# All left sides of a two-layer graph-attention kernel are turned through DRAM and VectorE's square transposes, and the hand-written order is made anew

## The chip, the cores and the metric

The kernel runs on one core of a Trainium2 chip. Such a core has a matrix engine (TensorE, "PE" in the profile, its weight loads "PEld"), a vector engine (VectorE, "DVE"), a scalar engine (ScalarE, "ACT"), a general engine (GpSimd, "POOL") and a sequencer that here issues the transfers (SyncE, "SP"). Each engine runs its own list of instructions strictly in the order in which they were written, and they meet only through semaphores. Transfers between DRAM and on-chip memory run on 16 DMA engines. The metric is the device time of one execution in microseconds (us); the number compared is the median of the runs.

## The reference

Two graph layers run over 64 graphs of 256 nodes with 512 features. Each layer normalizes its input, clips it at zero, and adds the result of an attention network over the graph's adjacency matrix:

```python
h = jnp.maximum(_layernorm(x, axis=-1), 0.0)
x = x + _L0_gnn_ref(adj, h, W1, att_src1, att_dst1, b1, W2, att_src2, att_dst2, b2)
h = jnp.maximum(_layernorm(x, axis=-1), 0.0)
x = x + _L1_gnn_ref(h, adj, W_proj, W_att, b_att)

def gat_layer(x, mask, W, a_src, a_dst, bias, concat):      # inside _L0_gnn_ref, called twice
    xl = (x @ W).reshape(B, N, H, F)
    e = leaky_relu(asrc[:, :, None, :] + adst[:, None, :, :], 0.2)
    attn = softmax(where(mask[..., None], e, -1e9), axis=1)
    out = einsum('bsdh,bshf->bdhf', attn, xl)
```

The first network has two such layers: 512 features to 4 heads of 256 (W1) with an ELU after it, then 1024 features to one head of 512 (W2). The second has one layer of 8 heads of 64 (W_proj), with the mask's rows and columns exchanged and a clip at zero at its end. Everything is float32.

## The kernel before

The graphs are independent and are worked on as a pipeline. The class `Graph` (L292) has one method for each small step, and three strings (`head`, `order`, `tail`, L638 to L690) name the steps in the order in which their instructions are recorded; `run` (L693) reads them. In an item such as `-1 gat3 0 1` the first number says which graph, counted from the round's number, and the rest is the method and its arguments. `order` runs once for each round from 2 to 62, so a steady round holds the steps of several graphs at different stages, one graph's worth in all. An item that begins with `w` prepares weights. This written order alone sets the place of every instruction on every engine; no scheduler moves anything (L125).

A graph's stages are, with their steps:

- `load` fetches x (tile `xs`, two buffers) and the adjacency `ad`; `stats1` and `norm1` make the normalized `h` on DVE, POOL and ACT; `masks` makes two 0/1 masks in bfloat16 from `ad` on DVE (L308, L310); `caps` turns one of them into limits on ACT, and `cap3` transposes it by DMA.
- `m1a`, `m1b` multiply h by the two halves of W1, `m2` the ELU's result z by W2, `m3` the second h by W_proj. Each is a `Product` (L38): a 2x2 blocked product with seven block products instead of eight, whose steps are p1, p2, p5, p6, p7, p4, p3 on PE, and c22. Four sums of blocks of the left side come first, from `left` on POOL (L212); the block products read the left side's seven blocks `a[:, i]`: p1 block 0, p2 block 1, p6, p5, p7 blocks 2, 3, 4 (the sums), p4 block 5, p3 block 6. ACT keeps partial sums (`kept`, L60) and DVE adds them (`total`, L260). The PSUM tiles are `sum` (two buffers) and `pm` (four).
- The attention's weights: `exp1`, `exp2`, `exp3` on ACT, then `rows1`, `rows2`, `rows3`, which call `spread` (L233): a small DVE transpose (L237), a write of 16 KB to DRAM, and reads that broadcast rows to all partitions (`bc`). `edges1`, `edges2`, `edges3` make the weight matrices `e` (ACT L289, then DVE L290), `gat1`, `gat2`, `gat3` multiply by them on PE, `out1`, `out2`, `out3` scale the results. `elu1` finishes the ELU of one half of z's columns for one half of the nodes: `elu1 g t` with g the columns' half and t the nodes' half. `store` writes the result.

A left side must lie with the features on the partitions, so it has to be turned. Before the change there are two ways. h of layer 1 (`away`, `back`) and the first half of z (`send2`, `back2`) take a trip: they are written to DRAM in blocks and read back rearranged, and DVE then transposes squares of 32x32 (`nc.vector.transpose`, L209, L430). The second half of z (`turn2`) and the h of layer 3 (`turn3`) are turned on PE with an identity (L196), and ACT copies them out of PSUM (L229, L441). The first and the last graph take PE for more. The read that ends a trip directly follows its write in SP's list, and so waits there until the write has landed:

```python
        kept = dram.tile([T, 4, P, P], F32, name="kept_h")
        nc.sync.dma_start(kept.rearrange("t a p e -> p t a e"), h.rearrange("p t (a e) -> p t a e", a=4))
        nc.sync.dma_start(h, kept.rearrange("t a (j q) e -> (a j) t (q e)", q=4))
```

`bias` adds b2 to `xs`, and `out2` adds the first network's result to it, into `x2` (two buffers), which `store` writes in the end.

## Time and profile before

| what | value |
|---|---|
| median of 3 runs | 3147.14 us (3146.95 to 3150.41) |
| span of the profiled execution | 3144.0 us; its own time is not listed apart from the runs |
| PE / DVE / ACT / POOL busy in the span | 97% / 78% / 60% / 40% |
| DMA engines, mean busy share in the middle | 39%, 112 GB/s |
| one round (one graph), from one step to the same step a graph later | 47.5 us |
| PE transposes in all | 1044 |

The span runs from the first to the last instruction. A busy share is an average over the span; what an engine is worth at some place is read from what waits there. In the groups by form a row shows line, engine, operation, tiles and shapes, the count, then after a bar the busy time in all and the mean duration in ns of one instruction, and after a second bar the idle time of the engine before these instructions with what ended it. Means of instructions that overlap with the next one are longer than what one of them costs; the distance between the starts of two steps in the timeline is the cost. In the timeline a row gives start, duration from the first start to the last end, engine, line and operation. SP's waits count from the end of its instruction before.

### The profile page before, as it was taken

How to read it: one execution, taken by the hardware profiler on the slowest of the kernel's cores; microseconds unless marked ns; L12 is line 12 of the kernel's file. 1: busy time of each engine (PE TensorE's matmuls, PEld its weight loads, DVE VectorE, ACT ScalarE, POOL GpSimd, SP SyncE). 2: the span in 40 equal slices, each digit the busy share in tenths (PEclk: the TensorE clock that was granted, in tenths of full speed). 3: DMA queues.
4: the chain of work that ended last, by engine and by line, in shares of the span. 5: the costliest groups of instructions: out<-in, count | busy, mean ns of one | idle time of the engine just before them, and what ended most of it. 6: DMA issues, size and time to landing. Idle time of an engine off the chain costs nothing. (4 is left out here: it accounts for less than half of the span.)

```text
span 3144.0 us, 60657 instructions
## 1 busy us (share of the span) xinstructions
PE 3064.8 (97%) x21312; PEld 2628.9 (84%) x21312; DVE 2466.5 (78%) x6503; ACT 1882.1 (60%) x4743; POOL 1245.5 (40%) x1434
## 2 busy tenths in 40 slices
PE   4899999999999999999999999999999999999997
PEld 3788888888888888888888888888888888888886
DVE  7588788787787787787787887887887877877875
ACT  2466666665666666566566666566666656666664
POOL 1443433433433434434434434434434334334342
PEclk8999999999999999999999999999999999999999
DMA  4234443333433433434433333433444334334331
GB/s 138 71 110 113 117 107 115 118 108 105 126 102 111 127 102 111 127 100 113 120 106 112 116 106 114 115 109 117 108 116 117 107 109 123 105 108 127 102 112 36
DMA packets 350779, 346.49 MB, mean 110 GB/s; under 512 B 78600, under 2 KB 236168, under 8 KB 350472
## 3 DMA queue, kind: packets, MB, share of 16 engines
q1 hardware_dynamic: 349096, 340.45, 37.6%
q8 instruction: 174, 2.85, 0.4%
q10 hardware_dynamic: 1376, 2.10, 0.2%
q14 instruction: 133, 1.09, 0.1%
HBM read 231.87 MB, written 102.20 MB: 106 GB/s over the span
## 5 line engine op out<-in xcount | busy, mean ns | idle before, releaser
L289 ACT ACTIVATE wy<-bc,exs_sb 128x256 f32<-128x256 f32 x1646 | 731.7, 500 | 261.7 <-DVE e L290 148.3
L260 DVE TENSOR_TENSOR xl<-pm,kept 128x256 f32<-128x256 f32 (+2 forms) x768 | 318.1, 421 | 414.6 <-PE pm L54 395.5
L60 ACT ACTIVATE kept<-sum 128x264 f32<-128x264 f32 (+3 forms) x768 | 294.4, 383 | 419.1 <-PE sum L54 416.2
L394 PE MATMUL pm<-xl,e 128*128 128x257 f32 x2048 | 498.6, 387 | 20.6 <-DVE e L290 15.1
L528 POOL TENSOR_TENSOR x<-x,o 128x256 f32<-128x256 f32 x256 | 196.4, 768 | 788.8 <-DVE o L526 770.2
L54 PE MATMUL sum<-w_sb,h1s 128*128 128x257 f32 x2048 | 489.7, 381 | 7.7 <-POOL h1s L216 7.1
L290 DVE SCALAR_TENSOR_TENSOR e<-wy,exs_sb,cap 128x256 f32<-128x256 f32 x1024 | 446.9, 479 | 56.0 <-ACT wy L289 56.0
L394 PEld LDWEIGHTS pm<-xl,e 128*128 128x128 f32 x2048 | 369.3, 190 | 100.2 <-PE pm L394 28.3
L54 PEld LDWEIGHTS sum<-w_sb,h1s 128*128 128x128 f32 x2048 | 380.6, 191 | 67.1 <-POOL h1s L216 7.5
L54 PE MATMUL pm<-w_sb,h1s 128*128 128x257 f32 x1536 | 365.4, 380 | 1.2 <-DVE xl L260 1.0
L181 POOL TENSOR_TENSOR rstd<-ve,neg_half 128x2 f32<-128x2 f32 x128 | 116.8, 912 | 622.0 <-DVE ve L179 622.0
L54 PEld LDWEIGHTS pm<-w_sb,h1s 128*128 128x128 f32 x1536 | 291.1, 190 | 45.4 <-issue 1.4
L290 DVE SCALAR_TENSOR_TENSOR e<-wy,exs_sb,mask 128x256 f32<-128x256 f32 x640 | 302.4, 523 | 5.2 <-ACT wy L289 5.2
L518 PEld LDWEIGHTS pm<-xl,e 128*64 128x64 f32 x8192 | 250.6, 138 | 47.3 <-issue 22.7
L54 PE MATMUL sum<-w1b_sb,hs 128*128 128x256 f32 x1024 | 266.7, 384 | 7.8 <-DVE w1b_sb L554 5.0
L54 PE MATMUL sum<-w1a_sb,hs 128*128 128x260 f32 x1024 | 268.7, 385 | 5.7 <-DVE w1a_sb L554 3.3
L54 PE MATMUL sum<-wp_sb,hs 128*128 128x264 f32 x1024 | 270.6, 387 | 3.0 <-ACT kept L60 2.5
L518 PE MATMUL pm<-xl,e 128*64 128x65 f32 x8192 | 269.2, 224 | 3.9 <-DVE e L290 2.9
L404 DVE SCALAR_TENSOR_TENSOR z<-pm,r,b_sb 128x256 f32<-128x256 f32 x512 | 247.8, 484 | 18.2
L466 PE MATMUL pm<-xl,e 128*128 128x257 f32 (+1 forms) x1024 | 242.6, 380 | 1.3 <-DVE e L290 1.3
L407 ACT ACTIVATE ez<-z 128x512 f32<-128x512 f32 x256 | 159.8, 624 | 125.0 <-DVE z L404 125.0
L54 PEld LDWEIGHTS sum<-w1b_sb,hs 128*128 128x128 f32 x1024 | 196.7, 193 | 36.9 <-issue 7.0
(103 smaller groups left out, 5076.3 us busy)
## 6 DMA issues: line engine op xcount, KB each, us to landing
bc<-kept SPq DMA_DIRECT2D x380, 256.0 KB
xs<-in_x_dram SPq DMA_DIRECT2D x64, 512.0 KB
out_dram<-x SPq DMA_DIRECT2D x64, 512.0 KB
kept_h<-h SPq DMA_DIRECT2D x63, 512.0 KB
h<-kept_h SPq DMA_DIRECT2D x63, 512.0 KB
kept_z<-z SPq DMA_DIRECT2D x124, 256.0 KB
z<-kept_z SPq DMA_DIRECT2D x124, 256.0 KB
ad<-in_adj_dram SPq DMA_DIRECT2D x64, 256.0 KB
```

The lines of the kernel that those rows point to most:

```text
L54: self.nc.tensor.matmul(to[:, :self.n], self.lhs[:, i, c, :], self.rhs[:, i, c, :], start=(first and c == 0), stop=(last and c == self.nk ...
L60: self.nc.scalar.activation(s[:, :self.n], self.sum[:, :self.n], AF.Copy)
L181: nc.gpsimd.tensor_tensor(rstd, ve[:, 0, :], neg_half, ALU.pow)
L260: nc.vector.tensor_tensor(dst, pm, add, ALU.add)
L289: nc.scalar.activation(wy, bc, AF.Copy, scale=yw)
L290: nc.vector.scalar_tensor_tensor(dst, wy, xw, mask, ALU.max, op)
L394: nc.tensor.matmul(pm[:, :Q + 1], self.e[1, h][:, s, t * P:(t + 1) * P], xl1[:, s, h, L1:], start=(s == 0), stop=(s == T - 1))
L404: nc.vector.scalar_tensor_tensor(z[:, sl], pm[:, :Q], r, b1_sb[:, sl], ALU.mult, ALU.add)
L407: nc.scalar.activation(ez, z[:, 2 * g * F1:2 * (g + 1) * F1], AF.Relu, scale=-1.0)
L466: nc.tensor.matmul(pm[:, :n], self.e[2][:, s, t * P:(t + 1) * P], xl2[:, s, half, L2:L2 + n], start=(s == 0), stop=(s == T - 1))
L518: nc.tensor.matmul(pv[q:q + 64, h, :], self.e[3, a * G + h][:, s, t * P + q:t * P + q + 64], xl3[:, s, a * G + h, :], start=(s == 0), stop ...
L528: nc.gpsimd.tensor_tensor(to, to, o.rearrange("p h k -> p (h k)"), ALU.add)
```

## The change

- Every left side of the graphs 1 to 62 now takes the trip through DRAM and DVE: `away3`, `home3` and `back` for the h of layer 3, and `send2`, `take2`, `back2` for both halves of z (`send2 g t` and so on, columns' half first). `turn` and `turn2` are gone; the graphs 0 and 63 are turned on PE through a `pm` tile.
- A trip's write and its read are steps of their own (`away1`/`home1`, `away3`/`home3`, `send2`/`take2`), and the row spreading is split into `ship` (transpose and write) and `rows` (reads).
- x is read a second time (`again`) into `x2`, which now has three buffers; `bias` adds b2 there, and `out2` adds into it. `xs` has one buffer.
- The second mask is made from `ad` by one scalar_tensor_tensor; `caps` writes over its own input. `cap` has three buffers.
- W1, W2 and W_proj are all brought in with the same layout of rows.
- `head`, `order` and `tail` are written anew. A round now reaches from `load` of its own graph (0) to `store` of the graph three before it (-3). The old and the new round are shown whole, of the two heads the parts up to and about the first W2 products; in the old head `dots2`, `columns2` and `sums2` (the columns and sums of W2) stand ahead of `edges1 0`. Renamed buffer counts are left out.

```diff
-    def turn(h, c, pt):
...
     def away(h):
         kept = dram.tile([T, 4, P, P], F32, name="kept_h")
         nc.sync.dma_start(kept.rearrange("t a p e -> p t a e"), h.rearrange("p t (a e) -> p t a e", a=4))
+        return kept
+
+    def home(h, kept):
         nc.sync.dma_start(h, kept.rearrange("t a (j q) e -> (a j) t (q e)", q=4))
...
         if gone:
             back(h, a)
         else:
-            for r in range(2):
-                pt = ps_tr.tile([P, 2, N], F32, name="pt")
-                turn(lambda t, c: h[:, t, c * P:(c + 1) * P], 2 * r, pt)
-                nc.scalar.activation(a[:, r:r + 5:4], pt.rearrange("p k (t q) -> p t k q", t=T), AF.Copy)
+            for t in range(T):
+                pm = ps_mm.tile([P, 512], F32, name="pm")
+                for c in range(DC):
+                    nc.tensor.transpose(pm[:, c * P:(c + 1) * P], h[:, t].rearrange("p (i c) -> p c i", c=DC)[:, c], ident)
+                nc.scalar.activation(a[:, 4 * t:4 * t + 2].rearrange("p r k m -> p (r k m)"), pm, AF.Copy)
...
-    def spread(w, heads):
-        wt = small.tile([P, 32], F32, name="wt")
+    def ship(w, heads):
+        wt = small.tile([P, 32], F32, name="wt", bufs=2)
         nc.vector.transpose(wt, w)
         kept = dram.tile([32, 4, 32], F32, name=f"kept{heads}")
         nc.sync.dma_start(kept.rearrange("c j i -> j c i"), wt)
+        return kept
+
+    def spread(kept, heads):
         rows = []
...
+            self.gone = 0 < b < B - 1
...
-            self.xs = io.tile([P, T, D], F32, name="xs")
+            self.xs = io.tile([P, T, D], F32, name="xs", bufs=1)
...
-            nc.vector.tensor_tensor(self.mask, a01, eye, ALU.max)
+            nc.vector.scalar_tensor_tensor(self.mask.rearrange("p t n -> p (t n)"), self.ad.rearrange("p t n -> p (t n)"), 0.0,
+                                           eye.rearrange("p t n -> p (t n)"), ALU.is_gt, ALU.max)
...
+        def again(self):
+            self.x2 = work.tile([P, T, D], F32, name="x2", bufs=3)
+            nc.sync.dma_start(self.x2, x[self.b].rearrange("(t p) d -> p t d", p=P))
+
         def bias(self):
-            nc.gpsimd.tensor_tensor(self.xs, self.xs, b2_sb[:, None, :].to_broadcast([P, T, D]), ALU.add)
+            nc.gpsimd.tensor_tensor(self.x2, self.x2, b2_sb[:, None, :].to_broadcast([P, T, D]), ALU.add)
...
-        def send2(self, t):
+        def send2(self, g, t):
+            if self.gone:
+                z = self.zt[t][:, g * (HF // 2):(g + 1) * (HF // 2)]
+                kept = self.e["kept", g, t] = dram.tile([4, P, P], F32, name="kept_z")
+                nc.sync.dma_start(kept.rearrange("a p e -> p a e"), z.rearrange("p (a e) -> p a e", a=4))
+
+        def take2(self, g, t):
+            if self.gone:
+                z = self.zt[t][:, g * (HF // 2):(g + 1) * (HF // 2)]
+                nc.sync.dma_start(z, self.e["kept", g, t].rearrange("a (j q) e -> (a j) (q e)", q=4))
+
+        def back2(self, g, t):
...
+            z, a = self.zt[t][:, g * (HF // 2):(g + 1) * (HF // 2)], self.a2[:, 4 * t + g]
+            if self.gone:
                 nc.vector.transpose(a.rearrange("p k (j q) -> p q k j", q=4), z.rearrange("p (q i c) -> p q c i", q=4, c=4))
...
-        def turn2(self, k):
...
+        def left2(self):
+            left(self.a2, HC // 2)
...
+        def away3(self):
+            if self.gone:
+                self.kept_h = away(self.h)
+
+        def home3(self):
+            if self.gone:
+                home(self.h, self.kept_h)
+
         def turn3(self):
-            self.m3 = Product(nc, ps_sum, ps_mm, work, left_of(self.h, False), wp_sb, put3)
+            self.m3 = Product(nc, ps_sum, ps_mm, work, left_of(self.h, self.gone), wp_sb, put3)
...
     head = """
...
-      m1a p1, w sums1 0, 0 m1a p6, w dots2 3, 0 m1a p7, w dots2 2, w dots2 7, w dots2 5, 0 m1a p5, 0 bias,
-      0 m1a p2, 0 m1a c22, w dots2 1, 0 m1a p3, 0 m1a p4, w dots2 4, w dots2 6, w columns2, 0 m1b p3, w
-      sums2 0, w sums2 1, 0 exp1, 0 rows1, w sums2 2, 0 caps, w sums2 3, 0 edges1 0, 0 edges1 3, 0 edges1
-      1, 0 edges1 2, 0 gat1 0 0, w load3, 0 cap3, 0 out1 0 0, 0 gat1 0 1, 0 out1 0 1, 0 gat1 1 0, 0 elu1 0
-      0, 0 send2 0, 0 out1 1 0, 0 elu1 0 1, 1 load, 0 send2 1, 0 elu1 1 0, 0 gat1 1 1, 0 back2 0, 0 out1 1
-      1, 0 back2 1, w dots3 7, 1 stats1, 1 masks, 0 elu1 1 1, 1 norm1, w dots3 1, 0 m2 p1, w dots3 2, w
-      dots3 0, 1 away1, w dots3 6, 0 turn2 0, 0 turn2 1, w dots3 5, 0 m2 p6, w dots3 4, w dots3 3, 1
...
+      0 m1a p2, 0 m1a p6, 0 m1a p5, w dots2 4, 0 m1a p7, 0 m1a c22, w dots2 1, 0 m1a p3, w dots3 0, 0 m1a p4,
+      0 exp1, w dots2 6, 0 ship1, 1 stats1, w dots2 0, 0 m1b p7, 0 m1b c22, 0 masks, w dots3 3, 0 rows1, 1 norm1,
+      0 edges1 0, 0 edges1 1, 0 send2 1 1, 0 m1b p3, 0 m1b p4, 0 edges1 2, 0 edges1 3, 0 caps, 0 gat1 0 0,
+      0 gat1 0 1, 0 out1 0 0, 0 out1 0 1, w dots2 3, 0 elu1 0 0, w dots3 7, 1 away1, 0 gat1 1 1, 0 out1 1 1,
+      0 gat1 1 0, 0 elu1 0 1, 1 home1, 0 send2 0 0, 0 cap3, 0 again, 0 out1 1 0, 0 back2 0 1, 0 elu1 1 1,
+      w dots2 2, 0 back2 1 1, 0 elu1 1 0, w dots2 7, w columns2, w dots3 4, 0 back2 0 0, w sums2 0, w sums2 1,
+      w dots3 2, 0 send2 0 1, w sums2 2, 0 back2 1 0, 0 m2 p1, 0 left2, w dots3 6, 0 take2 1 1, 0 take2 1 0,
+      0 m2 p2, 0 m2 p5, w sums2 3, w dots3 1, w dots3 5, 1 turn1, w sums3 0, w sums3 1, 0 m2 p6, 0 m2 p7, 0 bias,
+      0 take2 0 1, 0 m2 c22, 0 take2 0 0, w sums3 2, 1 masks, w sums3 3
...
     """
     order = """
-      0 gat1 0 0, 0 edges1 2, 0 out1 0 0, -2 gat3 1 1, 0 cap3, -1 stats3 1, -2 gat3 1 0, -1 norm3, -2 out3
-      1 1, 0 gat1 0 1, 0 elu1 0 0, 0 out1 0 1, 0 gat1 1 0, -1 turn3, 0 out1 1 0, 0 gat1 1 1, 0 elu1 0 1,
-      -1 m3 p1, 0 out1 1 1, 0 elu1 1 0, 0 send2 0, 1 stats1, -1 m3 p5, -1 m3 p6, 0 elu1 1 1, 0 back2 0, 0
-      send2 1, -2 out3 1 0, -1 m3 p2, 1 norm1, 1 away1, 0 back2 1, -2 store, -1 m3 p7, 0 turn2 0, 0 turn2
-      1, 0 m2 p1, -1 m3 p4, -1 m3 c22, 0 m2 p2, -1 m3 p3, 0 m2 p6, 1 masks, -1 exp3, 1 caps, 0 m2 p5, 1
-      bias, -1 rows3, 0 m2 p7, -2 range, 1 turn1, 1 m1a p1, 0 m2 p4, 0 m2 c22, 0 m2 p3, -1 edges3 1, 0
-      exp2, 0 rows2, 1 m1a p6, -1 edges3 0, 1 m1b p1, -1 edges3 5, 1 m1a p7, 1 m1a p5, 1 m1a c22, -1
-      edges3 4, 1 m1a p2, -1 edges3 2, 1 m1a p4, 1 m1a p3, -1 edges3 3, 1 exp1, 1 m1b p6, 1 rows1, -1
-      edges3 7, -1 gat3 0 0, -1 gat3 0 1, -1 out3 0 0, 0 edges2, -1 edges3 6, 1 m1b p5, -1 out3 0 1, 1 m1b
-      p7, 1 m1b c22, 1 m1b p2, 0 gat2 0, 0 out2 0, 0 stats3 0, 1 edges1 0, 1 m1b p3, 1 edges1 1, 1 m1b p4,
-      0 gat2 1, 0 out2 1, 1 edges1 3, 2 load
+      -3 edges3 5, -1 m1a p1, 0 load, -3 edges3 3, -2 m2 p4, -2 m2 p3, -2 exp2, -1 m1a p6, -2 ship2, -2 rows2,
+      -3 edges3 7, -3 edges3 1, -1 again, -1 m1a p5, -1 m1a p7, -1 m1a c22, -3 edges3 4, -3 edges3 6, -1 m1b p1,
+      -1 m1a p2, -1 m1a p3, -2 edges2, -1 m1a p4, -1 exp1, -1 m1b p6, -2 gat2 0, -1 caps, -1 ship1, 0 stats1,
+      -2 gat2 1, -1 rows1, -2 out2 0, -1 m1b p7, -2 out2 1, -2 stats3 0, -2 stats3 1, -3 gat3 0 0, -1 edges1 1,
+      -3 gat3 0 1, -1 m1b p5, -1 m1b c22, -1 cap3, -3 out3 0 0, -1 edges1 0, -1 m1b p2, -2 norm3, -1 edges1 2,
+      -2 away3, -1 edges1 3, -1 m1b p3, -2 home3, -1 m1b p4, -1 gat1 0 0, -1 out1 0 0, -1 gat1 0 1, -3 out3 0 1,
+      -1 gat1 1 1, -1 out1 0 1, -1 elu1 0 0, -1 out1 1 1, -1 elu1 0 1, -1 bias, -2 turn3, -1 gat1 1 0,
+      -1 send2 0 0, -3 gat3 1 1, -1 elu1 1 1, -1 send2 0 1, -2 m3 p1, -1 take2 0 0, -1 out1 1 0, -1 back2 0 0,
+      -3 gat3 1 0, -2 m3 p6, -1 send2 1 1, -3 out3 1 0, -1 elu1 1 0, -2 m3 p2, 0 norm1, -3 range, -1 take2 0 1,
+      -2 m3 p7, -2 m3 p5, -1 take2 1 1, -1 send2 1 0, 0 away1, -2 m3 p4, -1 back2 0 1, -1 take2 1 0, -2 m3 c22,
+      -1 back2 1 1, -2 m3 p3, -2 exp3, -2 ship3, -1 back2 1 0, 0 masks, -1 left2, -1 m2 p1, 0 home1, -3 out3 1 1,
+      -1 m2 p5, 0 turn1, -1 m2 p6, -1 m2 p2, -2 rows3, -2 edges3 0, -1 m2 p7, -2 edges3 2, -3 store, -1 m2 c22
     """
...
```

## The prediction

> **What bounds the kernel now.** I read the page's busy times first, then the windows, the groups by form, the timeline of one steady round, and the waits of the SP queue. From the page:
>
> ```profile
> span 3144.0 us, 60657 instructions
> PE 3064.8 (97%) x21312; PEld 2628.9 (84%) x21312; DVE 2466.5 (78%) x6503; ACT 1882.1 (60%) x4743; POOL 1245.5 (40%) x1434
> DMA  4234443333433433434433333433444334334331
> ```
>
> ```profile
> core 0: us, PE busy (x) PEld busy (x) DVE busy (x) ACT busy (x) POOL busy (x), PEclk, DMA share, GB/s
> 80.00:100.00 20.00, 17.25 (x71) 14.68 (x72) 9.21 (x17) 2.94 (x10) 15.45 (x16) 0.84 0.08 26
> 1000.00:2000.00 1000.00, 996.69 (x6975) 857.64 (x6974) 796.00 (x2080) 615.87 (x1555) 405.30 (x463) 1.00 0.39 112
> ```
>
> TensorE (PE) is busy 996.69 of 1000 us at clock 1.00 in the middle, so every us a graph takes off PE's list shows, as long as nothing else ends later. VectorE (DVE) has 20% to spare, the DMA engines 61%. The same step (the fourth W2 product) starts on PE at 999.96 and at 1047.46: a round, one graph, is 47.5 us, with 37.8 of DVE (796/1000 of it), 29.3 of ACT and 19.3 of POOL.
>
> The span is 3144.0; the runs' median is 3147.14 (3146.95 to 3150.41), so 3.1 us lie around the span. I predict on the median.
>
> ```profile
> L196 PE MATMUL pt<-ident,h 128*128 128x128 f32 x512 | 67.1, 274 | 3.4 <-ACT h L189 3.4
> L430 DVE STREAM_TRANSPOSE h1s<-z 128x512 f32<-128x512 f32 x124 | 143.2, 1154 | 0.8 <-DMA z<-kept_z 0.8
> L209 DVE STREAM_TRANSPOSE hs<-h 128x512 f32<-128x512 f32 x126 | 135.8, 1134 | 13.7 <-DMA h<-kept_h 11.5 <-POOL none L319 1.1
> L310 DVE TENSOR_TENSOR mask<-a,eye 128x512 bf16<-128x512 bf16 x64 | 85.2, 1332 | 2.2
> L308 DVE TENSOR_SCALAR a<-ad 128x512 bf16<-128x512 int32 x64 | 46.3, 724 | 0.0
> ```
>
> The timeline of PE in one round:
>
> ```profile
> 1028.16 1.04 PE L196 MATMUL pt<-ident,h 128*128 128x128 f32 x8
> 1029.04 1.90 PE L394 MATMUL pm<-xl,e 128*128 128x257 f32 x8
> 1035.22 1.04 PE L196 MATMUL pt<-ident,z 128*128 128x128 f32 x8
> 1036.10 1.91 PE L54 MATMUL sum<-w_sb,h1s 128*128 128x257 f32 x8
> ```
>
> And SP, which issues every transfer of a steady round in order (timeline, then its waits):
>
> ```profile
> 1026.50 0.38 SPq L424 DMA_DIRECT2D kept_z<-z  x1
> 1029.59 0.34 SPq L425 DMA_DIRECT2D z<-kept_z  x1
> SPq L244 <- DMA kept<-wt: 272.3, 190, 2.9
> SPq L425 <- DMA kept_z<-z: 269.9, 124, 3.2
> SPq L204 <- DMA kept_h<-h: 181.7, 63, 4.1
> ```
>
> **The change, part by part.**
>
> *PE loses turn2 and turn3.* Eight transposes take 0.88 us from their start to the next step's start (1028.16 to 1029.04, 1035.22 to 1036.10); the mean of 274 ns counts overlap. Two groups are 1.76 us a graph, and the floor of a round is 47.5 - 1.76 = 45.74. The built program's steady round holds no PE transpose; graphs 0 and 63 keep theirs. Over the 61 rounds of the list at most 61 x 1.76 = 107 us.
>
> The Trainium skill's "VectorE: DVE Perf Modes", section "Rules for kernel authors", speaks against the change: a 128x128 transpose belongs on TensorE where PSUM will do as its target, and "The three transpose paths" gives 390 ns for one there (bf16) and 311 ns on VectorE. By its 390 ns the 16 transposes would be worth an estimated 6.2 us a graph and 380 us in all. No sum here uses that: in this trace they cost 0.11 us each, issued back to back.
>
> *DVE gains four transposes of 128x512*: two at 1.154 (the second z halves) and two at 1.134 (h before layer 3): +4.6 us. The mask becomes one scalar_tensor_tensor from int32; no row shows that form. The bf16 form took 1.33, its fastest instance 0.42, the int32 comparison on the same tile 0.72. I take 0.72, the row that reads the same data: -0.6 (ends -0.9 and 0). DVE: 37.8 + 4.6 - 0.6 = 41.8 us, 90% of a round. ACT loses four evictions of 0.585: -2.3; the caps write in place at the same price. POOL keeps its work: bias moves to x2 and waits for the second read of x, which the list issues 21 us of PE work ahead.
>
> *DMA.* Two more z trips (0.25 MB out and back each), one h trip (0.5 MB), x again (0.5 MB): +2.6 MB on 5.3 a graph, so the share goes from 39% to about 60%. SP issues 28 transfers a round instead of 21; seven more at 0.4 us are 2.8 us of a queue that mostly waits. Reads stand apart from their writes, so SP no longer sits out a whole write. Behind a late take2 queue ship3, home1, rows3, and the store. xs has one buffer: the load waits for the previous norm1, half a round earlier, and stands 12 us of PE work ahead of stats1; at the crowded start such a load took 6.0 (issued 0.80, statistics at 6.79): hidden, and up to 6 us a round if it had no cover. x2 has three buffers: the second read waits for the store of three graphs before, a long time done.
>
> *What is late next.* Before, the trip carried only the first half of z, and the second went to PE directly. Now m2 p5, the second W2 product in the new list, needs a21 + a22 from POOL, and a22 is the z half that elu1 1 1 finishes. From the end of gat1 1 1 on PE: reciprocal and scaling 0.16 + 0.48; elu1 0 1, 0.72; the two transposes of turn3 that the list puts in front, 2.15 (the timeline's pair at 1044.66); elu1 1 1, 0.72; write leg 0.38 + 269.9/124 = 2.56; read leg, not shown by its landing: at least the small row write (0.52 + 272.3/190 = 1.95), at most the two row broadcasts for which ACT waited from 1013.11 to 1016.59, 3.5; nearest is the write of the same 256 KB, so 2.6; back2 1.15; left2's first addition 1.27. Sum 11.8, with some 0.4 of hand-overs 12.2. PE's cover between: gat1 1 0 1.74, two gat3 steps 2.0, seven m3 steps at 0.88 = 6.2, m2 p1 1.74: 11.7. PE waits about 0.5 there. On the way m3 p6 wants POOL's second addition after turn3: the same 0.5, not a second one, since it delays m2 p5 too.
>
> A second chain: the last W2 product to gat2 0, through put 0.43, exp 0.2, small transpose 0.2, row write 1.95, broadcast 2.6, weighting on ACT 0.5 and two on DVE 0.9: 6.8, with hand-overs 7.2, against eight products of 0.87 = 7.0: 0.2 waited. Before, that span held 3.7 us more (broadcast issued 1006.96, gat2 at 1015.23).
>
> Third, DVE may reach out1 late. Its own work from the last W2 put to out1 0 0 is 16.3 us by the timeline's pitches, against 17.7 on PE: enough. But edges1 hang on m1a p4: eviction 0.39, exp 0.2, small transpose 0.2, row write 1.95, two broadcasts 3.5, eight weightings on ACT at 0.42, norm3 in their midst 1.5, the last pair on DVE 0.9: 12.0, with hand-overs 12.4, against 11.6 of PE (six m1b products, gat2, two gat3 steps, half a gat1 step). So out1 0 0 starts 0.8 late, and DVE, which then has 4.8 of work for 5.0 of PE, is some 0.6 late at out1 1 1. How much of this adds to the first miss I bound by 0 and 0.6 and take the middle, 0.3.
>
> A round: 45.74 + 0.5 + 0.2 + 0.3 = 46.7, 0.8 less than now. 61 x 0.8 = 49.
>
> *Ends.* In the head PE idled 11.3 us before gat1 while DVE did the dots and the sums of W2 (four of 1.22 each), and 7.1 before an m2 product on POOL. The new head puts three dots2 steps, columns2 and the sums after edges1, 9 us of DVE, which m2 still needs: between 0 and 9 us won, I take 5. The last 37 us keep their chain (out2, norm3, m3, edges3, gat3): 0, within 5 either way.
>
> Sum: 3147.1 - 49 - 5 = 3093.
>
> **Rivals.**
> *Everything hidden.* If both legs stay at the fastest and DVE arrives on time, PE stays the bound: 3147 - 107 - 5 = 3035. For it: PE waits almost nothing today, and the z reads made DVE wait 0.8 us in 124. Against it: today's trips have more cover.
> *The trip sets the round (slower).* One mechanism: elu1 1 1 - trip - back2 - left2 - m2 p5. From 1.76 us of waiting a round on, nothing is won. The write legs reached 3.2 of wait (3.6 with issue) and kept_h's 4.1; with DMA at 60% and four trips plus two h trips crossing between turn3 and turn1, legs of 3.5 each instead of 2.6 add 1.8: 48.5 a round, 3147 + 61 - 5 = 3203; 0.8 added, 47.5, is the point of no change. At 48.0: 3147 + 30 - 5 = 3172.
> *DVE becomes the bound.* 41.8 us plus waits in its list; to reach 47.5 it needs 5.7 of idle. It idled 9.7 a round before, but for PE. I see some 4 (before the last W2 put, before the last take2): 45.8, below PE. Price if it does: 3147 to 3180.
> *The change doesn't do what it says.* Excluded for the transposes (the program's list); x's second read could delay out2, but has those 21 us.
>
> **How the numbers follow.** A difference under 0.2% (6.3 us) can't be told from none. Likeliest, 46.1 to 47.3 a round, 3055 to 3130: 0.43. Everything hidden, below 3055: 0.23. Trip or DVE as the bound beyond no change: 0.28 (trip 0.24, DVE 0.04). The rest, 0.06, lies near no change. Faster 0.66, same 0.05, slower 0.29. The likeliest case's own range is 3055 to 3130; the range that leaves two in ten out takes the floor, 3030, and the slower case to 3175. The number is the likeliest's.
>
> **What would show it.** Right: no L196 rows; a round of 46.7; PE waiting about 0.5 us a round for POOL h1s (left2's first addition) or hs; DVE near 90%; z read legs near 2.6. The hidden case: PE 99% in the middle with round 45.7. Wrong towards slower: PE idle before the w2 product on POOL h1s of 2 us and more, DVE waiting for DMA z<-kept_z, and write legs over 3 us. Wrong through DVE: PE waiting on DVE e or on DVE hs with DVE at 95%. The mask row tells 0.72 or 1.33.

## The result: 7.9% slower, with VectorE's operations longer beside POOL

The changed kernel takes 3393.07 us (median, 3389.6 to 3405.67) against 3147.97 for the kernel before: a ratio of 1.0785 (95% interval 1.0764 to 1.0805). The forecast was 3093, with 3175 as the upper end. The page of the changed kernel:

```profile
span 3403.6 us, 59370 instructions
PE 3051.1 (90%) x20320; PEld 2524.3 (74%) x20320; DVE 2972.3 (87%) x6751; ACT 1775.1 (52%) x4495; POOL 1258.7 (37%) x1434
```

The windows of the same run, with the columns of the prediction's fence (time, then busy us of PE, PEld, DVE, ACT and POOL, PE's clock, share of the DMA engines, GB/s):

```profile
1000.00:2000.00 1000.00, 906.04 (x6079) 749.65 (x6078) 880.57 (x1971) 526.90 (x1334) 371.39 (x422) 0.99 0.52 153
```

A round (the mean distance of one POOL instruction of the `caps` step, over 51 rounds in the middle) went from 47.55 to 52.09 us. 61 such rounds make 277 us more; the profiled spans differ by 259.6 (3403.6 against 3144.0), so head and tail together became 18 us shorter. (The profiled run, 3405.67, is the longest of the changed kernel's, 12.6 above the median; the mean clock granted to PE is 0.990 in it and 0.991 to 0.994 in the others.) PE is busy 94 us in 1000 less than before and waits instead; DVE is busy 880.57/1000 x 52.09 = 45.9 us a round, where the prediction had 41.8.

Which instructions hold the 4.1 us that were not foreseen? The groups by form of VectorE in the changed kernel:

```profile
L291 DVE SCALAR_TENSOR_TENSOR e<-wy,exs_sb,cap 128x256 f32<-128x256 f32 x1024 | 540.8, 588 | 58.2 <-ACT wy L290 58.0
L411 DVE SCALAR_TENSOR_TENSOR z<-ez,z 128x512 f32<-128x512 f32 x256 | 288.1, 1126 | 1.4 <-ACT ez L406 1.3
L432 DVE STREAM_TRANSPOSE h1s<-z 128x512 f32<-128x512 f32 x248 | 284.5, 1147 | 72.7 <-DMA z<-kept_z 70.2 <-POOL hs L213 1.6
L402 DVE SCALAR_TENSOR_TENSOR z<-pm,r,b_sb 128x256 f32<-128x256 f32 x512 | 247.8, 484 | 18.3
L313 DVE SCALAR_TENSOR_TENSOR mask<-ad,eye 128x512 bf16<-128x512 int32 x64 | 111.2, 1738 | 0.0
L501 DVE TENSOR_TENSOR lg<-lg,batt_sb 128x16 f32<-128x16 f32 x64 | 50.0, 782 | 0.3
```

and two of the same groups in the kernel before:

```profile
L290 DVE SCALAR_TENSOR_TENSOR e<-wy,exs_sb,cap 128x256 f32<-128x256 f32 x1024 | 446.9, 479 | 56.0 <-ACT wy L289 56.0
L413 DVE SCALAR_TENSOR_TENSOR z<-ez,z 128x512 f32<-128x512 f32 x256 | 184.3, 720 | 18.7 <-ACT ez L408 18.7
```

Nothing was changed in these lines of code: the count is the same, 1024 and 256, and yet the weightings cost (540.8 - 446.9)/64 = 1.5 us a graph more and the ELU's last operation (288.1 - 184.3)/64 = 1.6. The addition to the logits on 128x16 elements takes 0.782 us (0.168 before), and the new mask operation 1.738 where I had put 0.72. The transposes (1.147) and the operation that reads PSUM (L402, 0.484 in both kernels) did not move.

The timelines of DVE and of POOL show what the long ones stand beside. DVE first, then POOL:

```profile
1050.28 0.48 DVE L402 SCALAR_TENSOR_TENSOR z<-pm,r,b_sb 128x256 f32<-128x256 f32 x1
1050.68 2.56 DVE L411 SCALAR_TENSOR_TENSOR z<-ez,z 128x512 f32<-128x512 f32 x1
1054.35 0.68 DVE L411 SCALAR_TENSOR_TENSOR z<-ez,z 128x512 f32<-128x512 f32 x1
```

```profile
1050.34 2.35 POOL L354 TENSOR_TENSOR x<-x,b_sb 128x1024 f32<-128x1024 f32 x1
```

POOL's addition of b2 (`bias`) runs from 1050.34 to 1052.69. The ELU operation that starts in its midst ends at 1053.24, 0.55 us after it; the next one, with POOL idle, takes 0.68. So the first did not run slowly beside POOL, it stood until POOL was done. Between 300 and 2900 us, `e<-wy,exs_sb,cap` takes 0.479 us (median of 597) where no POOL addition runs at the same time and 0.938 (mean of 198) where one does; `z<-pm,r,b_sb`, with one operand in PSUM, takes 0.484 in both cases, and the reductions of `range` 0.297 and 0.298. It goes both ways: POOL's first addition after turn3, 0.73 alone, takes 1.00 where an ELU operation of DVE is under way.

The Trainium skill states this: "SBUF — State Buffer", section "Who interferes with whom", says that VectorE and GpSimd share a pair of ports by an exclusive lock, that a VectorE instruction with two inputs in SBUF, or a tensor_scalar in a fast mode, contends for it, and that the second to come is blocked until the first has finished. This case's rows agree on the two inputs and on the blocking, with 2.56 us for 0.68 in the row above; in which mode a tensor_scalar runs, no row shows. The prediction looked at POOL's queue only for what waits on its results.

Where PE waits in one steady round (timeline; in brackets the idle time and what ended it):

```profile
1053.99 1.15 PE L528 MATMUL pm<-xl,e 128*64 128x65 f32 x32 [0.62 <-DVE r L400]
1056.13 1.16 PE L54 MATMUL sum<-wp_sb,hs 128*128 128x264 f32 x4 [0.99 <-DVE hs L206]
1059.07 1.16 PE L54 MATMUL sum<-wp_sb,hs 128*128 128x264 f32 x4 [0.70 <-POOL hs L213]
1077.63 1.98 PE L54 MATMUL pm<-w_sb,h1s 128*128 128x257 f32 x8 [1.54 <-DVE xl L261]
1087.42 0.92 PE L464 MATMUL pm<-xl,e 128*128 128x257 f32 x3 [0.82 <-DVE e L291]
```

Each wait costs some 0.17 us more than its bracket, since the last matmul before it is counted to its end. By the starts of the steps the five come to 0.87, 1.12, 0.83, 1.70 and 0.98, 5.5 us. This round takes 51.77 (the m1b step ahead of it starts at 1039.22, the same step a graph later at 1090.99), so all that PE loses in it is 51.77 - 45.74 = 6.0, and small waits are the other 0.5. The mean round is 0.3 longer, most of it because in eight stretches of 3.4 us between 451 and 2230 us PE's granted clock is 0.5, and none of them lies in this round. The first two waits stand right behind the 2.56. The fourth is W2's last product (m2 p3), which waits until DVE has read c22's sum out of the same PSUM tile; that addition (1077.08) stands in DVE's queue behind four weightings (`edges3 0`, `edges3 2`) that run beside POOL's additions for turn1. DVE, then POOL:

```profile
1073.37 1.83 DVE L291 SCALAR_TENSOR_TENSOR e<-wy,exs_sb,cap 128x256 f32<-128x256 f32 x2
1075.76 1.39 DVE L291 SCALAR_TENSOR_TENSOR e<-wy,exs_sb,cap 128x256 f32<-128x256 f32 x2 [0.56 <-ACT wy L290]
1077.08 0.41 DVE L261 TENSOR_TENSOR xl<-pm,kept 128x257 f32<-128x257 f32 x1
```

```profile
1073.32 0.72 POOL L212 TENSOR_TENSOR hs<-hs 128x256 f32<-128x256 f32 x1 [1.38 <-DVE hs L206]
1074.13 0.79 POOL L213 TENSOR_TENSOR hs<-hs 128x256 f32<-128x256 f32 x1
1074.88 0.91 POOL L214 TENSOR_TENSOR hs<-hs 128x256 f32<-128x256 f32 x1
1075.75 0.72 POOL L215 TENSOR_TENSOR hs<-hs 128x256 f32<-128x256 f32 x1
```

The two pairs take 1.83 and 1.39, where a pair takes 0.87 in the kernel before; 0.56 of the delay is DVE waiting for ACT. None of the five is the wait for `left2`. The 0.5 that the prediction put there, or at m3 p6 as the same wait, shows at m3 p6 alone, as the third of the five, 0.83.

### The profile page after: what moved, and what is told of

The parts are those of the page before. It is cut to its first block, busy times and chain, and to the rows that moved or that the text cites. A ratio compares the mean times of both kernels' runs of the same rounds, so it can differ in the third digit from the quotient of the medians.

```text
span 3403.6 us, 59370 instructions
## 1 busy us (share of the span) xinstructions
PE 3051.1 (90%) x20320; PEld 2524.3 (74%) x20320; DVE 2972.3 (87%) x6751; ACT 1775.1 (52%) x4495; POOL 1258.7 (37%) x1434
## 4 chain that ended last, share of the span: by engine, by line
DVE 43%; DMA 25%; PE 23%; issue 5%; ACT 2%; POOL 1%; SPq 0%; DVEq 0%; ACTq 0%; POOLq 0%
DVE e L291 12%; DMA bc<-kept 8%; PE pm L54 8%; PE pm L464 7%; DMA z<-kept_z 6%; DVE z L411 6%; DMA kept_z<-z 6%; DVE hs L206 5%; DVE z L402 5%; PE sum L54 4%; DMA kept<-wt 4%; DVE xl L261 4%; PE pm L528 4%; DVE h1s L432 3%; DVE mask L313 2%
## 5 line engine op out<-in xcount | busy, mean ns | idle before, releaser
L290 ACT ACTIVATE wy<-bc,exs_sb 128x256 f32<-128x256 f32 x1646 | 745.3, 500 | 405.1 <-DMA bc<-kept 308.1
L291 DVE SCALAR_TENSOR_TENSOR e<-wy,exs_sb,cap 128x256 f32<-128x256 f32 x1024 | 540.8, 588 | 58.2 <-ACT wy L290 58.0
L392 PE MATMUL pm<-xl,e 128*128 128x257 f32 x2048 | 472.8, 383 | 15.7 <-DVE xl L261 15.2
L54 PE MATMUL pm<-w_sb,h1s 128*128 128x257 f32 x1536 | 379.6, 390 | 93.1 <-DVE xl L261 90.9
L392 PEld LDWEIGHTS pm<-xl,e 128*128 128x128 f32 x2048 | 383.3, 190 | 94.2 <-DVE xl L261 39.4
L538 POOL TENSOR_TENSOR x<-x,o 128x256 f32<-128x256 f32 x256 | 220.2, 861 | 467.2 <-DVE r L400 264.6
L432 DVE STREAM_TRANSPOSE h1s<-z 128x512 f32<-128x512 f32 x248 | 284.5, 1147 | 72.7 <-DMA z<-kept_z 70.2
L322 POOL TENSOR_SCALAR none<-deg 128x2 f32<-128x2 f32 x64 | 14.6, 228 | 759.7 <-ACT a L320 759.7
L54 PEld LDWEIGHTS sum<-wp_sb,hs 128*128 128x128 f32 x1024 | 183.7, 189 | 146.6 <-DVE hs L206 68.2
L411 DVE SCALAR_TENSOR_TENSOR z<-ez,z 128x512 f32<-128x512 f32 x256 | 288.1, 1126 | 1.4 <-ACT ez L406 1.3
L464 PE MATMUL pm<-xl,e 128*128 128x257 f32 (+1 forms) x1024 | 238.4, 385 | 46.0 <-DVE e L291 45.9
```

The lines of the kernel that those rows point to most:

```text
L54: self.nc.tensor.matmul(to[:, :self.n], self.lhs[:, i, c, :], self.rhs[:, i, c, :], start=(first and c == 0), stop=(last and c == self.nk ...
L290: nc.scalar.activation(wy, bc, AF.Copy, scale=yw)
L291: nc.vector.scalar_tensor_tensor(dst, wy, xw, mask, ALU.max, op)
L392: nc.tensor.matmul(pm[:, :Q + 1], self.e[1, h][:, s, t * P:(t + 1) * P], xl1[:, s, h, L1:], start=(s == 0), stop=(s == T - 1))
L411: nc.vector.scalar_tensor_tensor(z, self.e["ez", g, t], -1.0, z, ALU.add, ALU.max)
L432: nc.vector.transpose(a.rearrange("p k (j q) -> p q k j", q=4), z.rearrange("p (q i c) -> p q c i", q=4, c=4))
```

## Experiments

Theory 1: POOL's additions hold up DVE's operations with two on-chip operands, and DVE reaches PE's orders late. Theory 2: the trips through DRAM set the round. Theory 3: the new order makes PE wait, whatever the durations. The kernel before of each comparison took 3146.7 to 3148.7.

### One POOL step moved: e1_bias_later

```diff
-  -1 elu1 0 1, -1 bias, -2 turn3,
+  -1 elu1 0 1, -2 turn3,
...
-  -3 out3 1 0, -1 elu1 1 0,
+  -3 out3 1 0, -1 bias, -1 elu1 1 0,
```

> The changed kernel with one step moved: POOL's addition of b2 (bias) stands behind the third out3 instead of ahead of turn3, so it no longer runs beside the second elu1. Theory 1 (POOL's additions hold up those DVE operations that read two tensors from on-chip memory): the first elu1 row falls from a p90 of 2.57 us to 0.7, the mean of z<-ez,z from 1.15 to about 0.75, DVE gains 1.6 to 1.9 us a round ahead of turn3, and up to 61 x 1.85 = 113 us go: 3280, or 3335 if another wait takes half of it. Theory 2 (the trips' longer legs set the round): the elu1 rows may shorten, but the time stays at 3393 within 0.5%, since the reads still land when they did. Theory 3 (the order alone makes PE wait, whatever the durations): 3393 too, with the same elu1 rows.

Measured: 3279.77 (3277.03 to 3289.27), ratio 1.0436 (1.0418 to 1.0454): 113 us gone by moving one instruction a graph, which is theory 1's number. The group of the ELU operation, by form:

```profile
L411 DVE SCALAR_TENSOR_TENSOR z<-ez,z 128x512 f32<-128x512 f32 x256 | 174.9, 684 | 1.4 <-ACT ez L406 1.3
```

From 1126 to 684 ns, back below the kernel before; the round of the profiled runs falls from 52.09 to 49.98. PE's waits behind the ELU (`DVE r` and `DVE hs`) are gone from the list. The transfers are the same in number and size, so theory 2 falls for this part.

### The turns back on PE: e2_turns_on_pe

```diff
-            self.m3 = Product(nc, ps_sum, ps_mm, work, left_of(self.h, self.gone), wp_sb, put3)
+            self.m3 = Product(nc, ps_sum, ps_mm, work, left_of(self.h, False), wp_sb, put3)
...
         def away3(self):
-            if self.gone:
+            if False:
...
         def send2(self, g, t):
-            if self.gone:
+            if self.gone and g == 0:
...
```

> The changed kernel's order, with the h of layer 3 and the second halves of z turned on PE as in the kernel before (PE + 1.76 us a graph, DVE - 4.6, three trips fewer). Theory 2 (trips set the round): the waits go, the round falls to PE's 47.5 and some tenths, 3150 to 3180. Theory 1 (DVE, lengthened beside POOL, sets it): the stalls of elu1 by bias (1.85) and of edges3 by turn1's additions (1.4) stay, the waits for the total behind edges3 (1.7) and for the weights ahead of gat2 (1.0) stay; the round is 49.5 to 51, 3250 to 3345. Theory 3 (order alone): the waits of 6 us a round stay where they are and 1.76 comes on top: 53, 3460.

Measured: 3391.07 (3390.96 to 3392.52), ratio 1.0781: the same as the changed kernel, with three trips a graph fewer (`home3` is changed as `away3`, `take2` and `back2` as `send2`). Windows, and the first rows of PE's waits between 300 and 2900 us (us in total, times, longest):

```profile
1000.00:2000.00 1000.00, 940.98 (x6378) 793.49 (x6377) 791.00 (x1902) 562.99 (x1421) 381.09 (x426) 1.00 0.38 114
```

```profile
PE pm L392 <- DVE r L400: 71.2, 50, 1.4
PE pm L464 <- DVE e L291: 37.9, 51, 1.0
```

The DMA share is back at 0.38 and DVE at 791 us in 1000, and nothing is won: theory 2 falls for the three added trips. PE does 1.76 us more a round and waits that much less. What remains are waits for DVE behind the ELU operation held up by `bias` (the group still takes 1.16 us in the mean) and ahead of gat2. The number lies above theory 1's 3250 to 3345 and below theory 3's 3460. That turning on PE also takes buffers of `pm` between the products of the attention may have added to the first row; this was not separated.

### Weightings moved away from turn1's additions: e3_edges3_later and e6_bias_and_edges3

```diff
-  -2 m2 p4, -2 m2 p3, -2 exp2,
+  -2 m2 p4, -2 m2 p3, -3 edges3 0, -3 edges3 2, -2 exp2,
...
-  -2 rows3, -2 edges3 0, -1 m2 p7, -2 edges3 2, -3 store, -1 m2 c22
+  -2 rows3, -1 m2 p7, -3 store, -1 m2 c22
```

> The changed kernel with edges3 0 and edges3 2 moved behind the last W2 product (p3), so that DVE's partial sums of the W2 product no longer queue behind four weightings that run beside turn1's additions on POOL. Theories 1 and 3: the wait of PE for DVE xl ahead of m2 (1.7 us a round, 91 us in all) goes to 0.3 or less; 61 x 1.4 = 85 us off, 3308, or half of that (3350) if the delay comes back before gat2. Theory 2: no change, 3393 within 0.5%. What of DVE's rows stays long (e<-wy,exs_sb,cap at 0.94 beside POOL) says whether the port or the place made the wait.

Measured: 3360.63 (3359.25 to 3360.92), 32 us less than the changed kernel, not 85. Between 300 and 2900 us PE's wait for that sum went from 76.5 us to 0.8, as theories 1 and 3 had it, but the wait ahead of gat2 grew from 34.7 to 73.0 and the one for ACT's partial sums from 1.3 to 18.3: the weightings now stand ahead of `exp2` on ACT and DVE, and 55 of the 76 us came back there. The weightings fell from 588 to 533 ns.

With `bias` moved as well:

> Both moves together: bias behind the third out3 (alone: 3279.8) and edges3 0, 2 behind the last W2 product (alone: 3360.6). If the two stalls are separate places of one round, the gains add: 3393 - 113 - 32 = 3248. If the second one gave so little alone because elu1 beside bias took the time back, more comes: to 3393 - 113 - 85 = 3195. If both lie on one chain and only one counts: 3280.

Measured: 3256.17 (3254.2 to 3257.33), ratio 1.0346. 113 and 32 would give 3248; the two are separate and add, but for 8 us.

### The same hold-up put into the kernel before: e5_before_bias_at_elu and e11_before_bias_at_elu2

In the order of the kernel before, `bias` leaves its place beside the masks and goes ahead of the first ELU (e5):

```diff
-  -2 out3 1 1, 0 gat1 0 1,
+  -2 out3 1 1, 0 bias, 0 gat1 0 1,
...
-  0 m2 p5, 1 bias, -1 rows3,
+  0 m2 p5, -1 rows3,
```

or behind turn3's additions (e11):

```diff
-  -1 turn3, 0 out1 1 0,
+  -1 turn3, 0 bias, 0 out1 1 0,
...
-  0 m2 p5, 1 bias, -1 rows3,
+  0 m2 p5, -1 rows3,
```

> The kernel before with one step moved: POOL's addition of b2 stands beside the first elu1 (as it does in the changed kernel) instead of beside the masks. Theory 1: the row z<-ez,z rises from 0.72 us to about 1.15 on average, one instance in four to 2.3 to 2.6, and the mask row falls from 1.38 to 0.5 or less; DVE then reaches out1 and the first product of layer 3 later, so the time rises by between 0 (PE's list covers it) and 61 x 1.8 = 110 us: 3147 to 3257. If POOL does not hold up DVE: both rows as before, 3147 within 0.2%.

Measured: 3148.23, ratio 1.0004 (0.9994 to 1.0014). The test missed its aim: `bias` ran from 1028.74 to 1031.11, and the ELU operations came at 1027.37 and 1030.87, so only 0.2 us met (0.80 instead of 0.68). What it shows is that the place matters: the same step beside DVE operations that read PSUM costs nothing. The mask row stayed where it was (1.37 in this round, from 1044.33), because `left2`'s last addition (1043.97 to 1045.43), and not `bias`, was what held it.

> The kernel before with bias right behind turn3's additions on POOL, where the fourth elu1 follows on DVE within a microsecond. Theory 1: one elu1 in four takes 2.2 to 2.5 us and the mean of z<-ez,z rises from 0.72 to 1.05 or more; DVE idles 9.7 us a round there, so PE's list may cover it: 3147 to 3250. No hold-up by POOL: row and time as before.

Measured: 3257.62 (3257.16 to 3258.51), ratio 1.0348 (1.0331 to 1.0365). One instruction a graph moved on POOL makes the kernel before 109 us slower. The victim was another than expected. POOL, DVE and PE, one timeline each:

```profile
1018.45 2.35 POOL L362 TENSOR_TENSOR xs<-xs,b_sb 128x1024 f32<-128x1024 f32 x1
```

```profile
1018.86 1.97 DVE L178 TENSOR_SCALAR ve<-mv 128x2 f32<-128x2 f32 x1
1020.80 0.68 DVE L413 SCALAR_TENSOR_TENSOR z<-ez,z 128x512 f32<-128x512 f32 x1
```

```profile
1021.54 0.98 PE L196 MATMUL pt<-ident,z 128*128 128x128 f32 x7 [1.24 <-DVE z L413]
```

An operation on 128x2 numbers, 0.17 us by itself, stood for 1.97 until POOL's addition was over; the ELU behind it in DVE's queue, and PE's transposes behind that, came 1.8 late. The round went from 47.55 to 49.32: all of the 1.8 shows. So a PE that is 99.7% busy has no cover for a hold-up at that place, and a hold-up does not ask how large the victim is.

### More cover on PE, and the masks where POOL idles: e7_covers and e8_masks_early

e7 goes on from e6, with six buffers of `pm` (no step uses `pt` any more):

```diff
-  -1 m1b p6, -2 gat2 0,
+  -1 m1b p6, -1 m1b p7, -2 gat2 0,
...
-  -2 out2 0, -1 m1b p7, -2 out2 1,
+  -2 out2 0, -2 out2 1,
...
-  -3 gat3 1 0, -2 m3 p6, -1 send2 1 1,
+  -3 gat3 1 0, -2 m3 p2, -2 m3 p6, -1 send2 1 1,
...
-  -1 elu1 1 0, -2 m3 p2, 0 norm1,
+  -1 elu1 1 0, 0 norm1,
```

> The run before this with PE work put between two pairs: m1b p7 ahead of gat2 (0.87 us more cover for the weights of layer 2), m3 p2 between m3 p1 and m3 p6 (0.88 more cover for POOL's additions of layer 3), and the two PSUM banks that no step uses any more given to pm (six buffers instead of four). The two waits were 0.79 and 0.62 us a round in the run with bias moved. If order (place) makes them: 1.4 x 61 = 85 us off, 3160 to 3180. If DVE's and POOL's total work sets the round, they only move: within 20 us of the run before.

Measured: 3350.62, 94 us slower than e6. My own edit made a new wait. PE and ACT, from the timelines of one round:

```profile
1066.23 1.97 PE L54 MATMUL sum<-w1b_sb,hs 128*128 128x256 f32 x4 [2.18 <-ACT kept L60]
```

```profile
1064.39 0.91 ACT L289 ACTIVATE wy<-bc,exs_sb 128x256 f32<-128x256 f32 x2 [2.23 <-DMA bc<-kept]
1065.81 0.36 ACT L60 ACTIVATE kept<-sum 128x256 f32<-128x256 f32 x1
```

m1b p7 adds onto the PSUM tile that ACT must copy out after p6, and that copy stands in ACT's queue behind edges2's scaling, which waits for its rows from DRAM. This step tied PE to the very broadcast that it was to hide.

The wait is only part of the 94 us. The four matmuls behind it take 1.76 us to the next step (1066.23 to 1067.99) where such a step takes 0.87, and the window of the same stretch shows why (its last three numbers are PE's clock, DMA share and GB/s):

```profile
1066.40:1069.80 3.40, 3.40 (x9) 2.68 (x10) 1.29 (x6) 1.22 (x6) 0.31 (x2) 0.50 0.17 49
```

PE's granted clock is 0.50 there. The trace has 28 such stretches of 3.4 us between 110 and 3290 us, about one in two rounds, and e6 has none; the mean clock over the run is 0.980 against 0.994. At half the clock 28 x 1.7 = 48 us are lost, an estimate of about half of the 94. That the wait brings the stretch about is likely by its place, right behind the wait; no run tested it.

e8 is e7 with the masks moved:

```diff
-  -1 back2 1 0, 0 masks, -1 left2,
+  -1 back2 1 0, -1 left2,
...
-  -1 m1a p3, -2 edges2,
+  -1 m1a p3, -1 masks, -2 edges2,
```

> The run before this with the masks step moved from beside left2's additions on POOL to ahead of edges2, where POOL is idle and DVE waits. Theory 1: the mask row falls from 1.75 to 0.70 us and the comparison from 1.0 to 0.38, so DVE's busy time falls by 1.6 us a round; the time falls by between 0 and 61 x 1.6 = 98 us, by how much of it PE still waits for. If int32 data makes the mask operation slow, the row stays at 1.75.

Measured: 3351.25, no change, and the row is the reason to have run it. By form, between 300 and 2900 us:

```profile
L312 DVE SCALAR_TENSOR_TENSOR mask<-ad,eye 128x512 bf16<-128x512 int32 x50 | 34.1, 683 | 0.0
```

0.683 us instead of 1.754 in e7. The price that the prediction took for the new mask form, 0.72, is near the operation's own and wrong for its place. That it is near is luck: the row of the int32 comparison from which it came was itself held (0.73 beside POOL in the kernel before; 0.42 without, in e9). DVE's busy time fell from 843.75 to 806.18 us in 1000; PE waited on ACT as before, with 27 stretches at half the clock, so the time did not.

### A better order, and what turning is worth in it: e9, e10, e12, e13

e9 is e8 with cover that needs no ACT; m1b p7 is back behind `out2 0`, and m1b p5, gat3 0 0 and m3 p5 leave their later places:

```diff
-  -1 m1b p6, -1 m1b p7, -2 gat2 0,
+  -1 m1b p6, -1 m1b p5, -3 gat3 0 0, -2 gat2 0,
...
-  -3 gat3 1 0, -2 m3 p2, -2 m3 p6,
+  -3 gat3 1 0, -2 m3 p2, -2 m3 p5, -2 m3 p6,
...
-  -2 m3 p7, -2 m3 p5, -1 take2 1 1,
+  -2 m3 p7, -1 take2 1 1,
```

> The run with masks early, but with other PE work as cover: m1b p5 and gat3 0 0 (1.9 us, no ACT eviction among them) instead of m1b p7 ahead of gat2, and m3 p2, p5 ahead of m3 p6. The waits left in the run with bias and edges3 moved were 1.42 (gat2), 0.62 (POOL's second addition of layer 3), 0.38 (a partial sum of ACT) and 0.25 us a round, on a round of 49.3. If these places are all that is left: 45.74 + 0.6 to 1.3 = 46.3 to 47.0 a round, 3075 to 3120, faster than the kernel before. If DVE's and POOL's lists set the round in the end (their rows fall by 1.6 us by the masks): 48 to 48.5, 3180 to 3210. If m1b p5 repeats what m1b p7 did (PE behind an eviction that queues on ACT behind edges2): 3350.

Measured: 3264.43 (3261.09 to 3268.17), a round of 49.82: none of the three forecasts. The hold-ups are all but gone (0.489 us for the weightings, 0.689 for the ELU), DVE is down to 819.86 us in 1000, and gat2 waits no more; but m3 p6, p7 and p4 now stand side by side, and p7 and p4 must each wait until ACT has copied the sum before (0.53 and 0.51 in one round; for the first the profile names no releaser), m1b p3 waits 0.73 for a sum on DVE, m3 p1 0.45 for turn3. So theory 1 alone doesn't do: with the hold-ups away, the places of the steps still cost 4 us over PE's list.

e10 is e9 with the turns on PE, by the diff of e2:

> The same order with the h of layer 3 and the second halves of z turned on PE again: PE + 1.76 us a graph, DVE - 4.6. If PE is the bound in that order, this is what turning on VectorE is worth there: + 1.5 to 1.8 us a round, 90 to 110 us above the run before. If DVE is still the bound, this run is the faster one.

Measured: 3342.98 (3341.73 to 3345.1), 79 us slower than e9. In this order turning on VectorE is worth 79 of the 107 us that 1.76 x 61 make.

e12 rewrites the round, with e9's code (the masks early, six `pm`):

```diff
+  0 load, -3 edges3 5, -3 edges3 3, -3 edges3 0, -1 m1a p1, -2 m2 p4, -2 m2 p3, -2 exp2, -2 ship2, -1 masks, -1 m1a p6,
+  -1 m1a p5, -3 edges3 6, -3 edges3 2, -2 rows2, -1 m1a p7, -1 m1a c22, -3 edges3 1, -1 m1b p1, -3 edges3 4, -1 m1a p2,
+  -1 m1a p3, -3 edges3 7, -1 m1a p4, -2 edges2, -1 exp1, -1 m1b p5, -1 ship1, 0 stats1, -1 m1b p6, -2 gat2 0, -2 out2 0,
+  -2 gat2 1, -1 rows1, -2 out2 1, -1 caps, -2 stats3 0, -1 m1b p7, -2 stats3 1, -3 gat3 0 0, -1 m1b c22, -1 edges1 1,
+  -3 out3 0 0, -1 m1b p2, -1 again, -3 gat3 0 1, -1 m1b p3, -1 cap3, -2 norm3, -1 edges1 0, -1 edges1 2, -2 away3,
+  -1 edges1 3, -1 m1b p4, -1 gat1 0 0, -1 gat1 0 1, -1 out1 0 0, -1 out1 0 1, -1 elu1 0 0, -1 gat1 1 1, -3 gat3 1 1,
+  -1 gat1 1 0, -2 home3, -1 out1 1 1, -1 send2 0 0, -1 elu1 0 1, -2 turn3, 0 norm1, -2 m3 p1, -1 elu1 1 1, -1 send2 0 1,
+  -1 take2 0 0, -1 out1 1 0, -2 m3 p2, -1 send2 1 1, -3 gat3 1 0, -1 back2 0 0, -2 m3 p6, -1 take2 0 1, -1 elu1 1 0,
+  -3 out3 1 0, -1 back2 0 1, -1 take2 1 1, -2 m3 p5, -2 m3 p7, -1 send2 1 0, -1 bias, 0 away1, -2 m3 c22, -1 back2 1 1,
+  -1 m2 p1, -1 take2 1 0, 0 home1, -2 m3 p3, -2 m3 p4, -2 exp3, -2 ship3, -1 back2 1 0, -1 left2, -2 rows3, -1 m2 p5,
+  -3 out3 1 1, 0 turn1, -1 m2 p6, -1 m2 p2, -1 m2 p7, -3 out3 0 1, -1 m2 c22, -3 store, -3 range
```

> The changed kernel's work (no PE transposes, all trips kept) with the round written anew on top of the run with the good order: bias stands where DVE transposes, the masks where POOL idles, m1a p4 and exp1 no longer queue far behind edges2 on ACT, out1 follows gat1 in pairs, and POOL's additions for turn3 and left2 each have one DVE operation at most beside them that reads two on-chip tensors. If the hold-ups beside POOL and the queue behind edges2 are all that the changed kernel lost, the round comes to between PE's 45.74 and 47.2, and the time to 3040 to 3130: faster than the kernel before. If the trip chain (elu1 1 1, write, read, transposes, left2, m2 p5; 12.2 us by the prediction, 11.7 covered) sets the round once the rest is gone, 46.3 to 47.5: 3075 to 3147. If DVE's queue needs more than that whatever the order, 48 and more: 3180 or above, as in the run with the good order.

Measured: 3133.9 (3133.11 to 3143.41), ratio 0.9962 (0.9949 to 0.9976): with the same operations as the changed kernel in the same number, 259 us faster than it, and a little (0.4%) faster than the kernel before. It lies 4 us above the first forecast and within the second, whose chain over the trip, however, made PE wait only 0.2 us a round. Windows, PE's waits between 300 and 2900 us, and one group of DVE by form:

```profile
1000.00:2000.00 1000.00, 980.12 (x6624) 818.15 (x6623) 868.03 (x2156) 565.41 (x1460) 383.68 (x462) 1.00 0.57 167
```

```profile
PE sum L54 <- ACT kept L60: 14.5, 17, 1.6
PE pm L54 <- POOL h1s L211: 11.0, 52, 0.8
PE pm L391 <- DVE e L290: 10.1, 41, 0.4
```

```profile
L290 DVE SCALAR_TENSOR_TENSOR e<-wy,exs_sb,cap 128x256 f32<-128x256 f32 x1024 | 445.9, 492 | 55.9 <-ACT wy L289 46.4
```

DVE is at 868.03/1000 x 47.68 = 41.4 us a round, the prediction's 41.8, and the weightings cost what they did before the change. PE's waits come to 0.8 us a round; the second row is the wait for left2's first addition that the prediction put at 0.5 and that measures 11.0/54 = 0.2. In the profiled execution (3141.14, 7 us above the median) the round is 47.68, no shorter than the 47.55 of the kernel before: what makes it the faster one is the ends, 13 us shorter.

e13 is e12 with the turns on PE, by the diff of e2:

> The run before this with the h of layer 3 and the second halves of z turned on PE (1.76 us of PE a graph more, 4.6 of DVE and three trips less). In the good order the same exchange cost 79 us. If PE is near its bound in the run before, this one is 60 to 110 us slower than it; if the trips or DVE still set that round, it is equal or faster.

Measured: 3213.69 (3213.36 to 3214.24), ratio 1.0209 (1.0196 to 1.0223), 80 us slower than e12. In the orders of e9 and e12 turning on VectorE is worth 80 us; in the changed kernel's own order nothing that can be told from noise (e2). These orders were written for the trips: e13 has the PE work of the kernel before and PE waits only 0.4 us a round in it, and still its round is 48.96 against 47.55. So the 80 us are no gain over the kernel before. Each with an order of its own, e12 and the kernel before differ by 14.5 us.

## Why the prediction was wrong

- **PE's transposes.** Right: the steady round has none, and 1.76 us a graph left PE's list. In the orders of e9 and e12 it is worth 79 and 80 us of the 107.
- **DVE, "37.8 + 4.6 - 0.6 = 41.8".** This is the step that failed. The four transposes came as priced (1.147 and 1.118 against 1.154 and 1.134). But the sum took all other durations from the kernel before, as if an operation had one price. In their new places weightings, ELU, logits and mask stand beside POOL's additions, and the round holds 45.9 us of DVE. The moves say whose price was wrong: the mask is 0.683 with POOL idle and 1.754 beside left2, the ELU 0.684 and 1.126, and in e12 the sum of 41.8 is met (41.4). The sum that gives the time took its third wait from these prices, and so put 0.5 + 0.2 + 0.3 = 1.0 on PE's waits; they came to 6.0.
- **The warning was in the page.** The prediction quotes the old mask row with a mean of 1.33 and notes a fastest instance of 0.42. In that trace 62 of the 64 instances overlap a POOL addition and take 1.36 in the mean; the two that do not take 0.43. I used the row as a bound of a price without asking what stood beside it.
- **The three waits, 0.5 + 0.2 + 0.3.** The chain over the trip had no wait at m2 p5 in the changed kernel (0.2 in e12, when the rest is gone); the 0.5 showed at m3 p6, as 0.83. Write and read legs landed 2.4 and 2.9 us after their issue in the median, priced 2.56 and 2.6. The chain to gat2 was priced 7.2 us and measured 7.97 (1079.45 to 1087.42), because the row broadcast took from 1082.56 to 1086.34, 3.8 and not 2.6: 0.98 of wait instead of 0.2. DVE late, 0.3, became the two waits behind the ELU, 2.0, plus one that was not on the list at all: W2's last product behind the weightings, 1.7. Small waits add 0.5.
- **The rivals.** That the trip sets the round got 0.24 and was the case on the slow side; e2, without the three added trips, takes the same time and refutes it. That DVE becomes the bound got 0.04 and at most 3180; the late engine was DVE, by a mechanism that this rival didn't contain (it counted idle time in DVE's list, not longer operations). Its sign, PE waiting on `DVE e` and `DVE hs`, came true with DVE at 88%, not 95%.
- **Ends.** Predicted 5 us; by the difference of span and 61 rounds 18 in the changed kernel, and 18 to 21 in the runs made from it but e12 (13). Their cause stays open.
- **What is shown, and what is open.** Shown by one moved step each: `bias` beside the ELU, 113 us of the 245, and the same thing put into the kernel before, 109. That the 245 belong to the order and not to the turning or the added trips is shown by e12 (the same operations, 3133.9; it has two more buffers of `pm`, whose share was not measured alone) and by e2 (fewer trips, the same time). How the other 132 us divide between hold-ups (turn1's and left2's additions) and steps that simply stand too early or too late on ACT and DVE is open: e3 took 32 of it by a move that does both, e9 removed nearly all hold-ups and kept new waits, and no run took one without the other.

## What to carry to other kernels

Before a step is moved, lay the timelines of VectorE and GpSimd side by side: in these runs an operation of VectorE that reads two on-chip tensors, and a tensor_scalar down to 128x2 numbers, waited until GpSimd's addition was over, and GpSimd's additions waited for VectorE in turn, so a price read off one order did not hold in another. A row whose mean is far above its fastest instance may already stand beside something; find out what before the row is used. And cover for a wait has to be work that does not itself hang on the queue that is late.

## What the runs showed of the hardware that I had not expected

- A tensor_scalar on 128x2 numbers can stand for 1.97 us (0.17 alone) behind a GpSimd addition, and with it all that VectorE has queued. What passes, in the changed kernel between 300 and 2900 us, without and with a POOL addition beside it: operations with an operand in PSUM (0.484 and 0.484), reductions (0.297 and 0.298) and, nearly, the transposes of z (1.134 and 1.162 in the mean).
- PE loses time where the 64-column products of gat3 stand between full-width ones. From PE's timeline, first in e12, then in the kernel before:

```profile
1001.68 1.03 PE L54 MATMUL sum<-w1b_sb,hs 128*128 128x256 f32 x4
1002.63 1.15 PE L527 MATMUL pm<-xl,e 128*64 128x65 f32 x32
1003.72 1.13 PE L54 MATMUL pm<-w1b_sb,hs 128*128 128x256 f32 x4
1004.78 1.15 PE L527 MATMUL pm<-xl,e 128*64 128x65 f32 x32
1005.86 1.13 PE L54 MATMUL pm<-w1b_sb,hs 128*128 128x256 f32 x4
1006.83 1.03 PE L54 MATMUL sum<-w1b_sb,hs 128*128 128x256 f32 x4
```

```profile
1009.57 1.03 PE L54 MATMUL sum<-w1b_sb,hs 128*128 128x256 f32 x4
1010.52 2.09 PE L518 MATMUL pm<-xl,e 128*64 128x65 f32 x64
1012.54 1.13 PE L54 MATMUL pm<-w1b_sb,hs 128*128 128x256 f32 x4
1013.51 1.03 PE L54 MATMUL sum<-w1b_sb,hs 128*128 128x256 f32 x4
1014.37 1.03 PE L54 MATMUL pm<-w1b_sb,hs 128*128 128x256 f32 x4
```

Three m1b products and two gat3 steps take 5.15 us to the next start with the gat3 steps apart (1001.68 to 1006.83), and 4.80 with them together (1009.57 to 1014.37). e12 has both pairs of gat3 steps apart, the kernel before has them together; if the other pair costs the same, that is an estimated 0.7 us of the 1.9 by which e12's round misses 45.74. No run changed the pairing alone.
